# Values of two head pairs by seven products of blocks, and pairs that begin with the tokens the last one ended with

## The chip, the cores and the metric

The kernel runs on one core of one Trainium2 chip. The metric is the device time of one execution in microseconds, of which the median over several executions is taken; smaller is better. Everything is in 32-bit floats. In what follows PE is TensorE (the matmuls), PEld its loads of weights, DVE VectorE, ACT ScalarE, POOL GpSimd, and SP SyncE, whose queue issues most of the DMAs.

## What is computed

Two layers over x of shape (2, 512, 64, 32), that is two batches of 2048 tokens with 512 channels. Layer 0 is full softmax attention over eight heads of 64, whose queries and keys see an embedding of position beside the channels and whose values see the channels alone. Layer 1 is a Nystrom attention with a pseudo-inverse, followed by a linear map whose weights are looked up in a table of 16 levels. Only layer 0 is touched by the change:

```python
def _L0_conv_ref(hidden_states, Wq, Wk, Wv, Wout, bout):
    qk_hs = jnp.concatenate([hidden_states, emb], axis=1)
    qk_hs = qk_hs.reshape(B, -1, S).transpose(0, 2, 1)
    v_hs = hidden_states.reshape(B, C, S).transpose(0, 2, 1)
    q, k, v = qk_hs @ Wq, qk_hs @ Wk, v_hs @ Wv      # to 8 heads of 64
    scores = jnp.einsum('bhqd,bhkd->bhqk', q, k) * scale
    attn = jax.nn.softmax(scores, axis=-1)
    o = jnp.einsum('bhqk,bhkd->bhqd', attn, v)
    o = o.transpose(0, 2, 1, 3).reshape(B, S, HEADS * hd_v)
    o = o @ Wout + bout
    return o.transpose(0, 2, 1).reshape(B, C, H, W) + hidden_states
```

## The kernel before

**Tiling.** The unit of layer 0 is a pair of heads: 128 columns of each weight matrix. There are eight pairs, four for each batch, numbered 0 to 7 here and named (b, hp) in the code. The 2048 tokens of a batch stand in four blocks of 512 (`xbs`), channels in the partitions as four chunks of 128. A matmul of 32-bit floats shows as two instructions in the profile.

**Stages.** Stage n is `attention0` of pair n. It runs over 32 groups of two steps; a step is one block of 512 queries against 128 keys. For each step PE makes the scores (L1289), ACT the exponentials (L1297), DVE adds them up for the softmax's sums (L1307), and PE makes the product with the values (L1319) one group later. A block of queries ends every eight groups: ACT and DVE then read the two banks of the result out into the query tile (L1325, L1326), the next block's first product with the values needs the same two banks, PE sums the exponentials over the partitions (L805), DVE inverts (L1336), and SP spreads the inverse by eight DMAs (L816). The exponentials have six buffers, two for a group.

**What runs beside it.** The projections of pair n+1 are a generator, `Heads0.units`, that `attention0` advances in bursts: at the groups listed in `BURSTS[n]` it runs until the generator yields REST. Between bursts each group runs one thing: if the list `soon` holds a call, the first of it; otherwise, if the group stands in `TABLE[n]`, one step of `feed_forward_map`. That generator prepares layer 1's linear map in 84 steps: for each of four blocks the 16 levels, of which 14 cost two DVE instructions (L1397, L1398), and at the end four products on PE (L1411) and the load of the output weights `wo_f` into the buffer that these products read. Whatever is left of it after stage 3 is drained there, ahead of stage 4, whose burst at group 2 needs `wo_f`. `NVS` says how many steps run beside each block of values.

**Queries and keys by seven products.** For six of the eight pairs (all but (0,0) and (1,1), which are `plain`) `products` makes the queries and keys of two blocks of tokens by seven products of blocks where eight would be needed: the tokens' two halves of channels and two blocks of tokens are one 2x2 matrix of blocks, the key and query weights the other. It needs four sums of weights (`combine_w`, L1007 to L1010) and four sums of tokens (`Tokens.sum`, L917) for each half `tp` of the batch's tokens. The sums of tokens stand in four tiles (tags t5, t6, t7, t4) with one buffer each, so a half's sums replace the other's. `Tokens.begin` puts them on `soon`, or `need0` runs them when a product asks for one. Every pair goes through half 0, then half 1. The two banks of the tag "pp" hold a product that is read out by adds (`pc`) and a sum that stays in its bank over three products (`pu`).

**Values.** `values_of_tokens` (L1153) makes the values of one pair: for each block of 512 tokens four tiles of 128 tokens times four chunks of channels, with the tokens as PE's weights and 128 columns of the value weights moving; ACT copies the bank out (L1160). Per pair these are 64 matmuls, 128 instructions.

**Order.** PE, DVE, ACT and POOL run in the order in which the program is written; the order of SP's queue is made by the framework. A tag's buffers are given out as they come free. The tag "qo" has five, for the query tiles, which turn into the attention's output and stay until a batch's output projection; "k" and "v" have two each.

Of the kernel before, what the change touches and what calls it, by code (L numbers as in the profile page):

```python
# [37 lines left out]
def general_path(  # L38
# [636 lines left out]

PREFETCH = 26

TABLE = *[(1, 2, 3, 4, 5, 6, 7, 22, 23, 28)] * 3, (13, 14, 18, 19, 20, 21, 22, 23, 24, 26, 27, 28), (), (), (), ()
WAIT = 4
NVS = 3, 3, 3, 1  # L680
FEW = (2, 1), (1, 2), (1, 1), (2, 2)
BURSTS = (
    *[(9, 17, 25)] * 4, (2, 4, 7, 10, 12, 15, 18, 20, 23, 26, 28, 31),
    (9, 17, 25), (9, 17, 25), (9, 17),
)


# [1 line left out]
def fast_path(  # L689
# [63 lines left out]
    def chunked(ap):  # L753
        return ap.rearrange("(k p) n -> p k n", p=P)
# [64 lines left out]
    def advance(gens, n=1, whole=False):  # L819


        made, i = 0, 0
        while made < n and i < len(gens):
            got = next(gens[i], gens)
            if got is gens:
                gens.pop(i)
            elif got is GAP:
                i += 1
            elif got is REST:
                if whole:  # L830
                    break
            else:
                made += 1
        return made
# [53 lines left out]
    def blocks_of(w1, w2):  # L888

        lo, hi = slice(0, 2), slice(2, 4)  # L890
        return {1: w1[:, lo, :], 2: w1[:, hi, :], 4: w2[:, hi, :]}

    class Tokens:


# [6 lines left out]
        def begin(self):  # L902
            soon.extend(lambda m=m: self.sum(m) for m in (5, 6, 7, 4))
# [25 lines left out]
    def tokens_of(b, n, xbs, tp):  # L929
        return Tokens(f"{b}_{n}_{tp}", *xbs[2 * tp : 2 * tp + 2])  # L930

    class Heads0:


        def __init__(self, b, hp):
            self.b, self.hp = b, hp
            self.name = f"f0_{b}_{hp}"
            self.plain = (b, hp) in ((0, 0), (1, 1))
            self.n_units = 13 if b else 15 if self.plain else 14
            if self.plain:  # L940
                kinds = "qk" if b == 0 else "kq"
                self.uses = [(kind, t) for kind in kinds for t in range(NTB)]
            else:
                self.uses = [(kind, 2 * tp + t) for tp in range(2) for kind, t in (("k", 0), ("k", 1), ("q", 1), ("q", 0))]
            self.w, self.ws, self.e, self.ft = {}, {}, {}, {}

        def load(self, kinds="qk"):
            for kind in kinds:
                self.w[kind] = load_w0(kind, self.b, self.hp)

        def begin(self):
            self.k = kvpool.tile([P, S], F32, tag="k", name=f"k_{self.name}")
            self.v = kvpool.tile([P, NST, P], F32, tag="v", name=f"v_{self.name}")

        def queries(self):
# [43 lines left out]
        def combine_w(self):  # L999

            wk, wq = self.w["k"][0], self.w["q"][0]
            lo, hi = slice(0, 2), slice(2, 4)
            few = wpool0.tile([P, KC, P], F32, tag="s", name=f"s_{self.name}")
            s4 = wpool0.tile([P, 2, P], F32, tag="s4", name=f"s4_{self.name}")
            s1, s2, s3 = few[:, lo, :], few[:, hi, :], wq[:, lo, :]
            self.ws = {**blocks_of(wk, wq), 5: s1, 6: s2, 7: s3, 3: s4}
            nc.vector.tensor_tensor(s1, wq[:, lo, :], wq[:, hi, :], ALU.add)  # L1007
            nc.vector.tensor_tensor(s2, s1, wk[:, lo, :], ALU.subtract)
            nc.vector.tensor_tensor(s3, wk[:, lo, :], wq[:, lo, :], ALU.subtract)
            nc.vector.tensor_tensor(s4, wk[:, hi, :], s2, ALU.subtract)  # L1010

        def products(self, tp, part, after):

# [51 lines left out]
            yield  # L1065
            yield REST

        def values(self):
            for t in range(NTB):
                values_of_tokens(self.v, t, self.xbs[t], lambda k: self.w["v"][0][:, k, :], self.name)  # L1070
                yield

        def units(self, xbs, parts, after=None, ready=None):

            self.xbs = xbs
            self.begin()
            values = self.values()
            if self.b == 0 and self.plain:
                self.few("q")
                self.embed(4)  # L1080
                yield
            if self.plain:
                for i, (kind, t) in enumerate(self.uses):
                    if i == 2 and self.b == 0:
                        self.few("k")
                        self.embed(2)
                    if kind == "q" and self.b:
                        if t == 0:
                            yield from values
                            while not ready():  # L1090
                                yield GAP
                    if kind == "q" and t == 0:
                        self.queries()
                    self.project(kind, t)
                    yield
                if after:
                    after.begin()
            else:
                self.queries()
                if self.b and self.hp == 0:  # L1100
                    for m in range(2):
                        next(values)
                        advance(ffn_map, 3)
                        yield
                if not self.ws:
                    self.combine_w()
                    for _ in range(2):
                        next(values)
                        yield
                while ready and not ready():  # L1110
                    yield GAP
                for tp in range(2):
                    yield from self.products(tp, parts[tp], parts[1] if tp == 0 else after)
            if self.next:
                self.next.load()
                if self.next.b:
                    self.next.embed(4)
            for i, _ in enumerate(values):
                advance(ffn_map, NVS[i])
                yield  # L1120
                if self.next and not self.next.plain and not self.next.ws:
                    self.next.combine_w()
                if self.next and self.next.b == 0 and i == 2:
                    self.next.few("qk", nc.scalar.copy)
            if self.next:
                self.next.load("v")

            big = small.tile([P, 2], F32, tag="big0", name=f"big_{self.name}")
# [923 lines left out]
    made, plain = {}, lambda n: heads[n].plain  # L2052

    def parts_for(n):
        if n not in made:
            made[n] = [tokens_of(todo[n][0], n, xbs, tp) for tp in range(2)]
        return made[n]

    def units_of(n, ready=None):

        others = [m for m in range(n + 1, len(todo)) if todo[m][0] == todo[n][0] and not plain(m)]
        after = parts_for(others[0])[0] if others and not (n and plain(n)) else None
        return heads[n].units(xbs, None if plain(n) else parts_for(n), after, ready)

    loaded, ffn_map = [], [feed_forward_map()]
# [48 lines left out]
    def first_products():  # L2114
# [695 lines left out]
```

## Time and profile before

| what | value |
|---|---|
| median of 4 runs | 2650.52 us (2650.29 to 2650.92) |
| the profiled execution's own time | 2651.93 us |
| its span, first to last instruction | 2650.0 us |
| mean granted TensorE clock | 0.999 |
| scores L1289, 4096 instructions | 489.8 us busy |
| product with the values L1319, 4096 instructions | 494.1 us busy |
| values of layer 0, L1153 (vp_f), 1024 instructions | 117.9 us busy |
| sums of tokens L917, 48 instructions | 1218 ns each |
| adds of exponentials L1307 (two tiles), 448 instructions | 574.6 us busy |

The stages of layer 0 begin at 53.9, 207.3, 363.0, 515.8, 683.7, 904.0, 1056.6 and 1208.3 us, read from the first scores of each pair. Busy time of PE counts matmuls whose ends are modelled and overlap; durations of a group of matmuls are better read from the starts of the pieces in the chain of waits.

### The profile page before, as it was taken

The page shows a single profiled execution, that of the slowest core. Times are in us where ns is not written, and L with a number is a line of the kernel's source. Part 1 is how long each engine was busy: PE and PEld are TensorE (multiplying, and loading weights), DVE is VectorE, ACT ScalarE, POOL GpSimd, SP SyncE. Part 2 cuts the span into 40 slices and gives each one's busy share as a digit, 9 for nine tenths or more (in the row PEclk, how much of TensorE's full clock was granted, in tenths as well). Part 3 has the DMA queues.
Part 4 walks back from the last instruction along what each step waited for, and adds up shares of the span by engine and source line. Part 5 has one row for each costly group of instructions (what it writes and reads, how often), then busy time and mean ns, then how long its engine had stood idle before and what let it go on. Part 6 is the DMA issues. An engine that isn't in the chain of part 4 may idle for free.

```text
span 2650.0 us, 41440 instructions
## 1 busy us (share of the span) xinstructions
PE 2624.2 (99%) x16882; PEld 1353.5 (51%) x16882; DVE 1780.3 (67%) x2259; ACT 921.5 (35%) x1398; POOL 170.8 (6%) x127
## 2 busy tenths in 40 slices
PE   9999999999999999999999999999999999999998
PEld 5343443444344344353344555777677666665444
DVE  5788897886667777767868866544644645465665
ACT  1434453543344434435522323223333233231310
POOL 0011011000001100000002000000000000000000
PEclk9999999999999999999999999999999999999999
DMA  4001001201221201011115633213111113021211
GB/s 147 21 30 36 14 33 49 77 21 52 88 80 57 92 25 33 25 57 60 39 45 183 223 125 123 93 33 132 45 37 61 61 45 106 29 80 39 93 36 49
DMA packets 123609, 177.16 MB, mean 67 GB/s; under 512 B 16785, under 2 KB 77969, under 8 KB 120849
## 3 DMA queue, kind: packets, MB, share of 16 engines
q1 hardware_dynamic: 117264, 153.15, 17.6%
q0 software_dynamic: 5440, 20.97, 2.0%
q8 instruction: 134, 2.20, 0.3%
q14 instruction: 67, 0.54, 0.1%
q10 hardware_dynamic: 704, 0.31, 0.0%
HBM read 94.02 MB, written 63.57 MB: 59 GB/s over the span
## 4 chain that ended last, share of the span: by engine, by line
PE 92%; DVE 5%; issue 1%; ACT 1%; DMA 1%; SPq 0%; DVEq 0%; ACTq 0%
PE av_f L1319 15%; PE sc_f L1289 15%; PE pb L1866 5%; PE pa L1866 5%; PE vp_f L1153 4%; PE fp_g L2022 4%; PE yp_g L1168 4%; PE yp_f L1168 4%; PE vp L1153 4%; PE pc_f L1021 3%; PE pu L2207 3%; DVE acc_f L1307 2%; PE pu_f L1021 2%; PE sc L1695 2%; PE sc L1923 2%; PE av L1716 2%
## 5 line engine op out<-in xcount | busy, mean ns | idle before, releaser
L1297 ACT ACTIVATE p_f<-sc_f 128x1024 f32<-128x1024 f32 x512 | 496.7, 1022 | 539.9 <-PE sc_f L1289 539.8
L1307 DVE TENSOR_TENSOR acc_f<-acc_f,p_f 128x1024 f32<-128x1024 f32 x448 | 574.6, 1283 | 110.2 <-ACT p_f L1297 83.1
L1319 PE MATMUL av_f<-p_f,v_f 64*64 64x512 f32 x4096 | 494.1, 589 | 2.8 <-DVE q_f L1326 2.8
L1289 PE MATMUL sc_f<-q_f,k_f 64*64 64x512 f32 x4096 | 489.8, 591 | 0.3 <-ACT p_f L1297 0.3
L1319 PEld LDWEIGHTS av_f<-p_f,v_f 64*64 64x64 f32 x4096 | 162.4, 133 | 286.6 <-issue 274.1
L1289 PEld LDWEIGHTS sc_f<-q_f,k_f 64*64 64x64 f32 x4096 | 154.2, 133 | 282.2 <-issue 276.8
L1866 PE MATMUL pa<-M 128*128 128x192 f32 (+1 forms) x640 | 150.3, 380 | 0.0
L1866 PE MATMUL pb<-R 128*128 128x192 f32 (+1 forms) x640 | 149.3, 380 | 0.6 <-DVE M L1879 0.6
L1153 PEld LDWEIGHTS vp_f<-wv_f,x 128*128 128x128 f32 x1024 | 115.8, 192 | 5.5 <-issue 5.2
L1866 PEld LDWEIGHTS pb<-R 128*128 128x128 f32 x640 | 106.5, 190 | 23.6 <-DVE M L1879 0.8
L1866 PEld LDWEIGHTS pa<-M 128*128 128x128 f32 x640 | 108.2, 193 | 19.8 <-ACT M L1857 2.0
L1153 PE MATMUL vp_f<-wv_f,x 128*128 128x128 f32 x1024 | 117.9, 276 | 0.0
L1339 POOL TENSOR_TENSOR q_f<-q_f,rinv_f 128x512 f32<-128x512 f32 x32 | 51.9, 1621 | 968.1 <-DMA rinv_f<-acc_f 700.9
L1168 PE MATMUL yp_g<-o,wo_f 128*128 128x512 f32 x256 | 113.8, 595 | 0.0
L1168 PE MATMUL yp_f<-q_f,wo_f 128*128 128x512 f32 x256 | 112.4, 594 | 0.1
L1153 PE MATMUL vp<-w,xh 128*128 128x128 f32 x896 | 105.8, 276 | 0.0
L1153 PEld LDWEIGHTS vp<-w,xh 128*128 128x128 f32 x896 | 102.2, 192 | 5.4 <-issue 3.5
L1879 DVE SCALAR_TENSOR_TENSOR M<-M,pb 128x320 f32<-128x320 f32 (+1 forms) x160 | 60.1, 417 | 60.8 <-PE pb L1866 60.8
L2022 PE MATMUL fp_g<-xn_g,mT 128*128 128x512 f32 (+1 forms) x232 | 100.8, 586 | 0.0
L1928 ACT ACTIVATE p<-sc 128x512 f32<-128x512 f32 x128 | 66.7, 601 | 91.8 <-PE sc L1923 91.3
L1960 POOL TENSOR_TENSOR o<-o,rinv 128x512 f32<-128x512 f32 x32 | 44.5, 1389 | 774.8 <-DVE rinv L1959 573.9
L1879 DVE SCALAR_TENSOR_TENSOR R<-M,pa 128x320 f32<-128x320 f32 (+1 forms) x160 | 58.4, 406 | 42.0 <-PE pa L1866 42.0
(293 smaller groups left out, 3215.0 us busy)
## 6 DMA issues: line engine op xcount, KB each, us to landing
xh<-xh_fd SPq DMA_DIRECT2D x12, 1024.0 KB, 8.2
rinv_f<-acc_f SPq DMA_DIRECT2D x256, 32.0 KB, 1.9
xr_f<-in_x_dram SPq DMA_DIRECT2D x8, 1024.0 KB, 5.3
x_fd<-xr_f POOLq DMA_DIRECT2D x8, 1024.0 KB, 4.7
xh_fd<-xn_f POOLq DMA_DIRECT2D x8, 1024.0 KB, 4.4
k_fd<-kq SPq DMA_DIRECT2D x16, 512.0 KB, 2.6
q_fd<-kq SPq DMA_DIRECT2D x16, 512.0 KB, 3.1
k<-k_fd SPq DMA_DIRECT2D x8, 1024.0 KB, 6.0
```

The lines of the kernel that those rows point to most:

```text
L1021: nc.tensor.matmul(to, lhsT=w[:, k, :], rhs=x[:, k, :], start=start and k == 0, stop=k == 1, skip_group_check=True,)
L1153: nc.tensor.matmul(vp[:, j * P : (j + 1) * P], lhsT=xb[:, k, j * P : (j + 1) * P], rhs=w_of(k), start=k == 0, stop=k == KC - 1,)
L1168: nc.tensor.matmul(yp, lhsT=wo_sb[:, k, m * P : (m + 1) * P], rhs=oTs[k][:, toks], start=k == 0, stop=k == NPAIR - 1,)
L1289: nc.tensor.matmul(sc[r * D : (r + 1) * D, h, :], lhsT=hd.k[rows, lo : lo + D], rhs=hd.q[rows, t * TB : (t + 1) * TB], start=True, stop=True,)
L1297: nc.scalar.activation(p, sc, AF.Exp, scale=D**-0.5)
L1307: nc.vector.tensor_tensor(acc, first if c == 1 else acc, p, ALU.add)
L1319: nc.tensor.matmul(av[r][half, :], lhsT=hd.v[keys, c, half], rhs=pp[keys, h, :], start=c == 0, stop=c == NST - 1,)
L1866: nc.tensor.matmul(dst, lhsT=lhsT[:, k, t * P : (t + 1) * P], rhs=rhs[:, k, :], start=k == 0, stop=k == 1)
L1879: nc.vector.scalar_tensor_tensor(out, m, scale, pr, ALU.mult, ALU.subtract)
L1928: nc.scalar.activation(p[:, h, :], sc, AF.Exp, scale=D**-0.5)
L2022: nc.tensor.matmul(fp[:, cols], lhsT=mT[:, k, m * P : (m + 1) * P], rhs=self.xn[:, k, cols], start=k == 0, stop=k == KC - 1,)
L2207: nc.tensor.matmul(to, lhsT=w[:, k, :], rhs=x[:, k, :], start=start and k == 0, stop=k == 1, skip_group_check=True)
```

## The change

Four pairs of layer 0 are joined into two couples, (0,1) with (0,2) and (1,2) with (1,3). The first of a couple makes the values of both, again by seven products of blocks in place of eight: the tokens' blocks and their sums are those that its queries and keys use, and the value weights of the two pairs are the other matrix (`values_of_two`, `sums_of_blocks`, `combine_v`). The second has no values to make. The couple's two value weights, their sums, and the second pair's values stand in tiles of the tag "qo"; a tile of layer 1 that stood there moves to the tag "v". Each couple's products and values alternate by half, so that a half's sums serve both.

A pair now begins with the half of the tokens whose sums are still there: (0,2) and (1,2) go through half 1 first, and `parts_for` hands on the half that the pair before ended with. The last half of a pair therefore no longer starts the next pair's sums.

`TABLE` and `BURSTS` get other entries, and map steps run beside the couple's values, one for each of their units. The sums of weights of some pairs are put on `soon` in place of being made in a burst.

```diff
-TABLE = *[(1, 2, 3, 4, 5, 6, 7, 22, 23, 28)] * 3, (13, 14, 18, 19, 20, 21, 22, 23, 24, 26, 27, 28), (), (), (), ()
+TABLE = (1, 2, 3, 4, 6, 7), (1, 2, 3, 4, 5, 6, 7, 8, 10, 11, 12, 18, 19, 20, 21, 22, 23, 26, 27, 28), (1, 2, 3, 4, 5, 6, 7, 10, 11, 12, 20, 21, 22, 23, 24, 27, 28), (13, 14, 18, 19, 20, 21, 22, 23, 24, 26, 27, 28), (), (), (), ()
 BURSTS = (
-    *[(9, 17, 25)] * 4, (2, 4, 7, 10, 12, 15, 18, 20, 23, 26, 28, 31),
-    (9, 17, 25), (9, 17, 25), (9, 17),
+    (5, 9, 17, 25), (9, 17, 25), (9, 17, 25), (9, 17, 25), (2, 4, 7, 10, 12, 15, 18, 20, 23, 26, 28, 31),
+    (9, 14, 20, 25), (9, 17), (9, 17),
 )
+    def sums_of_blocks(w1, w2, few, s4):
+        lo, hi = slice(0, 2), slice(2, 4)
+        s1, s2, s3 = few[:, lo, :], few[:, hi, :], w2[:, lo, :]
+        nc.vector.tensor_tensor(s1, w2[:, lo, :], w2[:, hi, :], ALU.add)
+        nc.vector.tensor_tensor(s2, s1, w1[:, lo, :], ALU.subtract)
+        nc.vector.tensor_tensor(s3, w1[:, lo, :], w2[:, lo, :], ALU.subtract)
+        nc.vector.tensor_tensor(s4, w1[:, hi, :], s2, ALU.subtract)
+        return {**blocks_of(w1, w2), 5: s1, 6: s2, 7: s3, 3: s4}
...
+            self.couple = (b, hp) in ((0, 1), (1, 2))
+            self.coupled = (b, hp) in ((0, 2), (1, 3))
+            self.order = (1, 0) if (b, hp) in ((0, 2), (1, 2)) else (0, 1)
...
+        def load_v(self):
+            if self.couple:
+                w = qopool.tile([P, S], F32, tag="qo", name=f"wv_{self.name}")
+                w = w.rearrange("p (j k n) -> p j k n", j=4, k=KC)
+                for j in range(2):
+                    cols = slice((self.hp + j) * P, (self.hp + j + 1) * P)
+                    nc.sync.dma_start(w[:, j], chunked(wv0[:, cols]))
+                w1, w2, few, s4 = (w[:, j] for j in range(4))
+                self.vs = (w1, w2, few, s4[:, :2, :])
+                self.wvs = {}
+            elif not self.coupled:
+                self.load("v")
...
         def begin(self):
             self.k = kvpool.tile([P, S], F32, tag="k", name=f"k_{self.name}")
+            if self.coupled:
+                return
+            if self.couple:
+                v = qopool.tile([P, S], F32, tag="qo", name=f"v_{self.next.name}")
+                self.next.v = v.rearrange("p (c d) -> p c d", d=P)
...
+        def values_of_two(self, tp, part, after):
...
+            def product(to, m, start=True):
+                while m not in part.of or m not in self.wvs:
+                    soon.pop(0)()
+                w, x = self.wvs[m], part.of[m]
+                for j in range(TB // P):
+                    cols = slice(j * P, (j + 1) * P)
+                    for k in range(2):
+                        nc.tensor.matmul(
+                            to[:, cols], lhsT=x[:, k, cols], rhs=w[:, k, :],
+                            start=start and j + k == 0, stop=k == 1, skip_group_check=True,
+                        )
...
+            def begin(i, t, bank):
+                nc.scalar.copy(piece(i, t), blocks(bank))
+            def add(i, t, bank):
+                d = piece(i, t)
+                nc.vector.tensor_tensor(d, blocks(bank), d, ALU.add)
+            pc = other(2)
+            begin(0, 0, pc)
+            pu = bank(f"pu_{name}")
+            product(pu, 1)
+            add(0, 0, pu)
+            yield
+            pc = other(5)
+            begin(0, 1, pc)
+            begin(1, 1, pc)
+            product(pu, 6, False)
+            add(0, 1, pu)
+            yield
+            pc = other(3)
+            add(0, 1, pc)
+            product(pu, 7, False)
+            add(1, 1, pu)
+            yield
+            pc = other(4)
+            begin(1, 0, pc)
+            add(1, 0, pu)
+            if after:
+                after.begin()
+            yield
+            yield REST
...
-                for tp in range(2):
-                    yield from self.products(tp, parts[tp], parts[1] if tp == 0 else after)
+                if self.couple:
+                    soon.append(self.combine_v)
+                for tp in self.order:
+                    then = parts[1 - tp] if tp == self.order[0] else after
+                    steps = self.products(tp, parts[tp], None if self.couple else then)
+                    if self.coupled and tp != self.order[0]:
+                        steps = (step for step in steps if step is not REST)
+                    yield from steps
+                    if self.couple:
+                        values = self.values_of_two(tp, parts[tp], then)
+                        if tp == self.order[0]:
+                            for step in values:
+                                if step is not REST:
+                                    advance(ffn_map, 1)
+                                yield step
             if self.next:
                 self.next.load()
                 if self.next.b:
                     self.next.embed(4)
-            for i, _ in enumerate(values):
-                advance(ffn_map, NVS[i])
+                if not self.next.ws and not self.next.plain and (self.coupled or self.b and self.plain):
+                    soon.append(self.next.combine_w)
+            if self.coupled:
+                values = ()
+            if self.coupled and self.next:
+                yield REST
+                self.next.few("qk", nc.scalar.copy)
+                yield
+            for i, step in enumerate(values):
+                if step is REST:
+                    continue
+                advance(ffn_map, 1 if self.couple else NVS[i])
                 yield
...
             if self.next:
-                self.next.load("v")
+                self.next.load_v()
...
     def parts_for(n):
         if n not in made:
             made[n] = [tokens_of(todo[n][0], n, xbs, tp) for tp in range(2)]
+            before = [m for m in made if m < n and todo[m][0] == todo[n][0]]
+            if before:
+                tp = heads[n].order[0]
+                made[n][tp] = made[before[-1]][tp]
         return made[n]
...
-        others = [m for m in range(n + 1, len(todo)) if todo[m][0] == todo[n][0] and not plain(m)]
-        after = parts_for(others[0])[0] if others and not (n and plain(n)) else None
+        after = parts_for(1)[0] if n == 0 else None
...
             else:
-                d = qopool.tile([P, S], F32, tag="qo", name=f"kq_{pair.name}_{tp}")
+                d = kvpool.tile([P, S], F32, tag="v", name=f"kq_{pair.name}_{tp}")
```

More of the change, by code (lines that the diff above doesn't have):

```diff
@@ L943, in __init__ @@
             else:
-                self.uses = [(kind, 2 * tp + t) for tp in range(2) for kind, t in (("k", 0), ("k", 1), ("q", 1), ("q", 0))]
+                self.uses = [(kind, 2 * tp + t) for tp in self.order for kind, t in (("k", 0), ("k", 1), ("q", 1), ("q", 0))]
             self.w, self.ws, self.e, self.ft = {}, {}, {}, {}
@@ L1004, in combine_w, with combine_v @@
             s4 = wpool0.tile([P, 2, P], F32, tag="s4", name=f"s4_{self.name}")
[L1005 to L1010, printed above, removed]
+            self.ws = sums_of_blocks(wk, wq, few, s4)
+        def combine_v(self):
+            self.wvs = sums_of_blocks(*self.vs)
         def products(self, tp, part, after):
@@ L1066, in products, with other, piece, blocks @@
             yield REST
+        def values_of_two(self, tp, part, after):
+            name = f"v_{self.name}_{tp}"
+            def product(to, m, start=True):
[9 more added lines that the diff above has]
+                        )
+            def other(m):
+                to = bank(f"pc{m}_{name}")
+                product(to, m)
+                return to
+            def piece(i, t):
+                v, t = (self.next.v if i else self.v), t + 2 * tp
+                return v[:, 4 * t : 4 * t + 4, :]
+            def blocks(bank):
+                return bank.rearrange("p (j d) -> p j d", d=P)
+            def begin(i, t, bank):
[27 more added lines that the diff above has]
+            yield REST
         def values(self):
```

## The prediction

> **What bounds the kernel now.** I read the page first: the busy shares, the slices, the shares of the chain that ended last.
>
> ```profile
> PE 2624.2 (99%) x16882; PEld 1353.5 (51%) x16882; DVE 1780.3 (67%) x2259; ACT 921.5 (35%) x1398; POOL 170.8 (6%) x127
> ...
> DVE  5788897886667777767868866544644645465665
> ...
> PE 92%; DVE 5%; issue 1%; ACT 1%; DMA 1%; SPq 0%; DVEq 0%; ACTq 0%
> ```
>
> TensorE (PE) is busy all the time and makes up 92% of the chain; VectorE (DVE) is the second load, nowhere denser than in layer 0 (the first 18 slices). Since ends of matmuls are modelled, I take rates from the chain in order of time, where each piece starts where the last one let it:
>
> ```profile
> 247.53 1.72 PE pc_f L1021 x4
> 249.25 1.72 PE pu_f L1021 x4
> ...
> 326.48 10.93 PE vp_f L1153 x96
> 338.67 3.77 PE vp_f L1153 x32
> 342.44 1.88 PE sc_f L1289 x16
> 344.31 1.72 PE av_f L1319 x16
> ...
> 480.69 14.49 PE vp_f L1153 x128
> ```
>
> A pair's values (vp_f, 128 instructions) cost 14.49 us, 113.2 ns each, and nothing stands between them. One of the seven products (four instructions over 512 columns) takes 1.72 us, 429 ns for four times the columns; so 128 columns cost about a quarter of 512, and TensorE goes by columns. Removing a column removes time, as long as VectorE doesn't take over. Whether it can, the windows by stage say. Stage n is the attention of pair n with the projections of pair n+1 beside it; columns: stretch, length, then busy us of PE, PEld, DVE, ACT, POOL.
>
> ```profile
> 53.90:207.30 153.40, 151.65 (x1221) 64.31 (x1224) 127.89 (x136) 68.26 (x77) 17.18 (x12) 1.00 0.11 34
> 207.30:363.00 155.70, 154.10 (x1248) 65.49 (x1244) 133.41 (x145) 68.64 (x78) 18.40 (x12) 1.00 0.09 28
> 363.00:515.80 152.80, 152.04 (x1248) 64.83 (x1244) 129.34 (x143) 68.26 (x76) 10.80 (x8) 1.00 0.17 54
> 515.80:683.70 167.90, 167.29 (x1280) 70.37 (x1276) 124.56 (x128) 70.71 (x80) 6.59 (x4) 1.00 0.16 50
> ...
> 904.00:1056.60 152.60, 152.60 (x1241) 64.68 (x1244) 121.16 (x110) 68.26 (x76) 11.06 (x6) 1.00 0.13 37
> 1056.60:1208.30 151.70, 151.70 (x1244) 64.61 (x1240) 106.02 (x93) 68.26 (x76) 6.04 (x6) 1.00 0.15 49
> ```
>
> VectorE fills 83 to 86% of stages 0 to 2 (127.89/153.40, 133.41/155.70). It is no bound on the average, but it runs in order, and where it is late at the wrong moment TensorE stops. The timeline of stage 0 shows the one kind of place:
>
> ```profile
> 165.34 0.42 DVE L1397 TENSOR_SCALAR hits_f<-tmp_f 128x512 f32<-128x512 f32 x1
> ...
> 165.79 0.69 DVE L1398 TENSOR_TENSOR wl_f<-wl_f,hits_f 128x512 f32<-128x512 f32 x1
> 166.21 1.03 PE L1319 MATMUL av_f<-p_f,v_f 64*64 64x512 f32 x4
> 166.40 1.22 DVE L1307 TENSOR_TENSOR acc_f<-p_f,p_f 128x1024 f32<-128x1024 f32 x1
> 167.54 0.68 DVE L1326 TENSOR_TENSOR q_f<-av_f,q_f 128x512 f32<-128x512 f32 x1
> 168.28 1.93 PE L1319 MATMUL av_f<-p_f,v_f 64*64 64x512 f32 x12 [1.04 <-DVE q_f L1326]
> ```
>
> At the switch from one 512-token block to the next, the attention's values need the bank that q_f (L1326) reads out. A map step (L1397, L1398) stood ahead of it on VectorE, and TensorE waited: 16 instructions and their switch take 1.90 us in undisturbed rows, here 166.21 to 170.14 (where the sums L805 start), so 2.0 us were lost. The same happens at 323.98 and 639.14.
>
> **The change, part by part.**
>
> (1) Values of two pairs. Removed for each couple: 2 pairs x 128 = 256 instructions. Added: 2 halves of the tokens x 7 products x 4 token tiles x 2 chunks x 2 passes = 224, of the same form. For two couples that is 64 fewer x 113.2 ns = **-7.25 us**. By stage: stages 0 and 5 gain 96 x 113.2 ns = 10.9 us, stages 1 and 6 lose 14.5 us. A product now ends every 16 instructions, a block before every 32. What such a hand-over costs the trace doesn't show for 128 columns. Below: nothing, since L1021's products follow each other at 4 x 429 ns, with the same two banks. Above: what the entry into a burst costs, 1.91 - 1.72 = 0.19 us (pc_f at 284.31 against its neighbours), for 28 products, 5.3 us. I take +0.3, near the L1021 rows.
>
> (2) Its VectorE and ScalarE work. Per couple 10 adds from a bank at 692 ns (L1041, the same shapes) = 6.9 us, and 4 sums of weights at 417 to 426 ns = 1.7 us; ScalarE keeps 8 copies of 586 ns. All of it lies beside products of 1.8 us each: between two uses of a bank there is always one whole product, and the longest read-out of a bank is two copies, 1.2 us. Nothing on the path; without that cover 0.6 us per hand-over.
>
> (3) Tokens kept. Pairs 2, 3, 6, 7 start with the half that the last ended with, so 4 x 4 token sums (L917, 1218 ns) go: 19.5 us of VectorE, against (2) 17.2 us. These sums fill stages 0, 1, 3 and 5 in the groups after a burst, so what they free is slack, not path, except at the switch above.
>
> (4) Map steps moved. A step is about 0.45 + 0.71 = 1.15 us (L1397, L1398). Counting the groups in which something in `soon` comes first: before, stages 0 to 3 take 16, 20, 20, 18 of the 84 steps after 10 ahead of stage 0; after, 9, 14, 24, 22. VectorE by stage, from the windows: stage 0: 127.9 - 4.9 (sums) + 8.6 (2) - 7 x 1.15 = 124 of 163; stage 1: 133.4 - 4.9 - 6 x 1.15 = 122 of 141; stage 2: 129.3 + 4 x 1.15 = 134 of 153; stages 5 and 6 under 125 of 163 and 101 of 137. The fullest is 88%. In stage 0 nothing is left in groups 18 to 24 ahead of the last switch, so the 2.0 us at 168.28 goes: **-2.0**, and with no step at group 28 most of the 0.48 us that the sums waited for VectorE at 211.41: **-0.4**. Late next there is only the exp's own add. In stage 1 the sums of weights and five steps stand where four sums and two steps stood: the stall of 323.98 stays, between -0.5 and +0.5, take 0. Stage 2 now has four steps ahead of its last switch: 0 to +1.0, take +0.2. In stage 0 the sums of the values' weights and a step follow a burst just before the first switch: 0 to +1.0, take +0.3.
>
> (5) Bursts. Stages 0 and 5 have four instead of three, stage 6 two: one more in all. Stage 1's third holds only two small embedding products, which before sat among the values. Entry 0.19 + exit (1.88 - 1.72) 0.16 = **+0.35**.
>
> (6) The map's own products. My count leaves five steps, four products and the last, for the drain at the end of stage 3 (before: 648.83 and 666.25). TensorE does them either way. But they now stand right ahead of stage 4, and the load of wo_f, which writes where they read, is issued after them, behind or beside the 1 MB store of the product (landing 6.7 and 8.5 us). The first yp_f comes 11.1 us after the stage's first scores (683.66 to 694.80), so 6.7 + 0.4 is hidden; xr_f, queued on SP behind the store, lands at 0.6 + 8.5 + 4.9 = 14 us and is needed at 11.1 + 3.7. Margins of 4 and 1 us: 0 to +3 if SP's queue puts the eight rinv_f pieces (4.9 us) ahead; take +0.3.
>
> (7) Buffers. The couple's weights and the second pair's values stand among the q tiles, layer 1's first kq in a v tile: slots that nobody waits for in the trace. 0.
>
> **Sum.** -7.25 + 0.3 - 2.0 - 0.4 + 0.2 + 0.3 + 0.35 + 0.3 = **-8.2 us**. The profiled execution took 2651.93 us (span 2650.0 and 1.9 around it), so 2643.7; it lies 1.4 above the median of the runs, so **2642.3** for the median.
>
> [...]
>
> **Rivals.**
>
> *A, it is given back (nothing to measure).* Stage 1 loses its whole burst of values, the stretch in which ten map steps ran beside 14.5 us of TensorE; now all its steps share groups with the adds. A group gives VectorE 3.43 us and asks 2 x 1.28 + 1.15 = 3.7, so each step adds 0.27 us of lag; eight in a row give 2. If the first switches of stages 1 and 2 and the last of stage 2 stall for 1 us each, and wo_f or xr_f costs 3 at stage 4: -8.2 + 6 = -2.2, **2648.3**. Against it: stages 1 and 2 have seven such steps in a row already, and their first switch shows 0.2 us (16 av_f instructions in 1.93 instead of 1.72 us at 241.40).
>
> *B, VectorE becomes the bound of layer 0 (slower).* The place is the switch again: four in each of stages 0 to 3, three of the 16 stall now. If lag is never worked off, all stall at 2.0 us each: 13 x 2.0 = 26, with (1) alone kept, 2650.5 - 7.25 + 26 = **2669**. It decides from (5.3 + 7.25) / 2.0, some six new stalls. For it: the fuller map steps and the lost burst. Against it: 122 to 134 us of work in 141 to 163.
>
> *C, banks (slower).* If every new product waits for the copy before it, 28 x 0.59 = 16.5: 2658.8. L1021's products, with longer read-outs (2 x 0.69 us), show no gap.
>
> **How the numbers follow.** The forecast (faster by over 0.2%, that is under 2645.2; 0.2% is about what runs of this kernel can tell from no change) gets 0.80, A 0.13, B 0.05, C 0.02. The forecast's own range: the low ends (no hand-over cost, -0.5 in stage 1, no other stall) give 2640.5, and another stall may go with the sums, so 2639.5; the high ends of (4) and (6) together 2647. The whole range is 2639.5 to 2647: it holds the forecast and the nearer part of A. Faster 0.80, same 0.13, slower 0.07.
>
> **What would show it.** Values instructions down from 1024 to 960, 448 of them in the new products, and L917 from 48 to 32. Stage 0 near 162 us, stage 1 near 141, 5 near 163, 6 near 137. No wait of av_f on q_f at stage 0's last switch. Wrong would be: pieces of the new products above 1.85 us (step 1), waits of av_f on VectorE in stages 1 and 2 above 1 us (step 4), yp_f or the first residual waiting for a DMA at stage 4 (step 6).

## The result, and the profile after

The changed kernel takes 2652.9 us (median of 40 runs, 2650.62 to 2656.29) against 2650.28 for the kernel before (60 runs beside them, 2648.4 to 2652.5): ratio 1.0011, 95% interval 1.0007 to 1.0016. It is slower by 2.6 us, where 8.2 us less were forecast. Its profiled span is 2653.0 us, at a mean granted clock of 0.997 (before 0.999); that execution took 2654.88 us, 2.0 above the median, and what follows on stages and waits is read from it.

The page of the changed kernel: busy shares, the slices of VectorE, the shares of the chain that ended last.

```profile
PE 2622.1 (99%) x16818; PEld 1351.4 (51%) x16818; DVE 1783.5 (67%) x2271; ACT 921.1 (35%) x1398; POOL 172.3 (6%) x127
...
DVE  5769897988467766787867866644644645465665
...
PE 93%; DVE 5%; ACT 1%; DMA 1%; issue 1%; SPq 0%; DVEq 0%; ACTq 0%
```

The 64 instructions are gone (16818 for 16882) and little else on this page moves: the page can't show where the time went. The windows by stage can (stretch, length, busy us of PE, PEld, DVE, ACT, POOL, granted clock, DMA share, GB/s).

```profile
54.00:217.00 163.00, 162.33 (x1317) 75.21 (x1320) 122.11 (x126) 70.58 (x81) 14.41 (x11) 1.00 0.07 23
217.00:360.80 143.80, 139.88 (x1124) 51.01 (x1120) 125.25 (x130) 66.37 (x74) 19.73 (x14) 1.00 0.10 34
360.80:515.30 154.50, 152.85 (x1248) 64.59 (x1244) 132.41 (x151) 68.24 (x76) 11.35 (x8) 1.00 0.18 56
515.30:682.10 166.80, 166.80 (x1276) 70.71 (x1268) 131.72 (x148) 69.99 (x79) 7.14 (x4) 1.00 0.11 31
902.50:1074.00 171.50, 168.44 (x1337) 76.69 (x1340) 125.21 (x119) 70.59 (x80) 11.03 (x6) 0.97 0.11 32
1074.00:1211.50 137.50, 137.50 (x1116) 52.99 (x1112) 107.80 (x95) 65.89 (x72) 6.77 (x5) 1.00 0.18 54
```

Taken from the first scores of each pair, the lengths of stages 0 to 6 and of the rest are:

| kernel | 0 | 1 | 2 | 3 | 4 | 5 | 6 | rest |
|---|---|---|---|---|---|---|---|---|
| before | 153.5 | 155.7 | 152.7 | 167.9 | 220.3 | 152.7 | 151.7 | 1441.7 |
| after | 163.1 | 143.7 | 154.5 | 166.9 | 220.4 | 171.5 | 137.5 | 1441.5 |

Stages 0, 3, 4 and 6 are near what was forecast (162, no change, no change, 137), stages 1 and 2 are 2.5 and 1.5 us longer than forecast, and stage 5 is 8 us longer (171.5 for 163). It is also the one whose clock is not 1.00. The signs of being wrong that the prediction named did not show: behind the first product of each block the new products take 1.79 us, av_f waits in stages 1 and 2 for 0.52 us at most, and TensorE shows no wait in stage 4. The time went where no sign had been set.

**The new products are as cheap as forecast.** Pieces of the chain of waits in order of time (start, us):

```profile
184.32 1.79 PE pu_v_f L1109 x16
186.11 1.79 PE pc_v_f L1109 x16
187.89 1.79 PE pu_v_f L1109 x16
```

Each starts where the one before let it: 1.79 us for 16 instructions, 111.9 ns each, no hand-over. (The first of each of the four blocks takes 1.98, the entry that step (5) priced at 0.19; the one behind the embedding products takes 2.00.)

**Stage 5.** The timeline of the changed kernel at its first block of queries (start, us, engine, line, operation, in brackets the idle time before and its releaser):

```profile
914.72 1.22 DVE L1344 TENSOR_TENSOR xn_f<-xn_f,rstd_n 128x1024 f32<-128x1024 f32 x1
...
915.69 1.38 POOL L1452 TENSOR_TENSOR q_f<-q_f,rinv_f 128x512 f32<-128x512 f32 x1 [35.72 <-DMA rinv_f<-acc_f]
915.85 5.60 DVE L1420 TENSOR_TENSOR acc_f<-acc_f,p_f 128x1024 f32<-128x1024 f32 x2
...
917.03 3.34 POOL L1343 TENSOR_TENSOR xn_f<-xn_f,rstd_n 128x1024 f32<-128x1024 f32 x1
...
921.38 0.41 DVE L897 TENSOR_TENSOR s_f<-wq_f 128x256 f32<-128x256 f32 x1
...
922.50 0.42 DVE L900 TENSOR_TENSOR s_f<-wk_f,s_f 128x256 f32<-128x256 f32 x1
...
925.30 2.28 DVE L1244 TENSOR_REDUCE big_f<-k_f 128x1 f32<-128x2048 f32 x1
...
939.27 0.68 DVE L1439 TENSOR_TENSOR q_f<-av_f,q_f 128x512 f32<-128x512 f32 x1
...
940.01 3.68 PE L1432 MATMUL av_f<-p_f,v_f 64*64 64x512 f32 x12 [3.06 <-DVE q_f L1439]
```

And the kernel before at the same place:

```profile
918.82 2.20 POOL L1339 TENSOR_TENSOR q_f<-q_f,rinv_f 128x512 f32<-128x512 f32 x1 [36.28 <-DVE acc_f L1307]
...
917.32 2.55 DVE L1307 TENSOR_TENSOR acc_f<-acc_f,p_f 128x1024 f32<-128x1024 f32 x2
...
919.79 2.28 DVE L1131 TENSOR_REDUCE big_f<-k_f 128x1 f32<-128x2048 f32 x1
...
922.10 1.25 DVE L1136 SCALAR_TENSOR_TENSOR bound<-big_f 128x1 f32<-128x1 f32 x1
...
937.38 2.79 PE L1319 MATMUL av_f<-p_f,v_f 64*64 64x512 f32 x16
...
937.50 0.69 DVE L1326 TENSOR_TENSOR q_f<-av_f,q_f 128x512 f32<-128x512 f32 x1
```

Two things load VectorE more ahead of the first switch. The four sums of the query and key weights (L897 to L900, 921.38 to 922.92) now stand on `soon` here. And the two multiplications of GpSimd (L1452, L1343) now run beside two adds of exponentials, which take 5.60 us in place of 2.55; before, they began at 918.82 and met the reduction, which kept its 2.28 us, and the small bound operation (1.25 us for 0.16). In this stage a group asks VectorE for two adds, 2.66 us, and gives it 3.43, so that only 0.77 us of lag is worked off in each. Counted from the stage's first scores, VectorE reads the bank out at 36.76 us, before at 33.52. At the switch, TensorE (PE) is idle for 3.06 us; the kernel before shows no idle row there, though its 16 instructions take 2.79 us for the 1.90 of undisturbed rows. Then something is late that no count of instructions shows; granted clock in the column before the last two:

```profile
936.00:938.00 2.00, 0.94 (x8) 0.06 (x2) 1.90 (x2) 1.24 (x2) 0.00 (x0) 1.00 0.00 0
938.00:940.00 2.00, 0.00 (x0) 0.00 (x0) 2.00 (x4) 0.00 (x0) 0.00 (x0) 0.78 0.00 0
940.00:942.00 2.00, 1.99 (x10) 0.77 (x12) 1.90 (x2) 0.00 (x0) 0.00 (x0) 0.50 0.00 0
...
946.00:948.00 2.00, 2.00 (x3) 0.67 (x2) 0.00 (x0) 0.00 (x0) 0.00 (x0) 0.50 0.00 0
...
950.00:952.00 2.00, 2.00 (x6) 0.95 (x5) 0.69 (x1) 0.00 (x0) 0.00 (x0) 1.00 0.48 131
```

The clock falls to half at about 939.1 and comes back at about 949.3: 10.2 us, in which the 12 instructions take 3.68 us (1.93 at the full clock).

**Stage 0's end**, the second place. The timeline of the changed kernel around the last burst of stage 0:

```profile
197.12 0.69 DVE L1131 TENSOR_TENSOR v_f<-pu_v_f,v_f 128x512 f32<-128x512 f32 x1 [2.01 <-ACT v_f L1127]
...
198.79 2.28 DVE L1244 TENSOR_REDUCE big_f<-q_f 128x1 f32<-128x2048 f32 x1
...
200.99 1.74 DVE L1449 RECIPROCAL acc_f<-acc_f 128x256 f32<-128x256 f32 x1
...
207.44 16.70 DVE L1420 TENSOR_TENSOR acc_f<-acc_f,p_f 128x1024 f32<-128x1024 f32 x10
...
212.41 4.01 POOL L1013 TENSOR_TENSOR e_k_f<-ft_k_f 128x512 f32<-128x512 f32 x2
...
224.19 0.64 PE L805 MATMUL rs_f<-acc_f,ones 128*32 128x256 f32 x8 [3.53 <-DVE acc_f L1420]
```

The last add of the values ends at 197.8, after the burst's last product (from 196.40 PE is at scores again), and a map step, the queries' reduction and the reciprocal, which the program puts behind it, are done at 202.7, with the exponentials' adds waiting. GpSimd's multiplication at 210.36 and its embedding adds (L1013, 2.0 us each) then slow the adds: ten take 16.70 us where 13.2 would do (1.33 us from one to the next). The embedding adds end at 220.4, just ahead of the sums; in the kernel before the same four end at 202.6, 8.8 us ahead of them. The sums wait 3.53 us; before 0.48:

```profile
211.41 0.64 PE L805 MATMUL rs_f<-acc_f,ones 128*32 128x256 f32 x8 [0.48 <-DVE acc_f L1307]
```

The wait forecast to go, av_f on q_f at stage 0's last switch, is gone.

### The profile page after: what moved, and what is told of

Read it like the earlier page. It is cut to its first block, busy times and chain, and to the rows that moved or that the text cites. A ratio compares the mean times of both kernels' runs of the same rounds, so it can differ in the third digit from the quotient of the medians.

```text
span 2653.0 us, 41334 instructions
## 1 busy us (share of the span) xinstructions
PE 2622.1 (99%) x16818; PEld 1351.4 (51%) x16818; DVE 1783.5 (67%) x2271; ACT 921.1 (35%) x1398; POOL 172.3 (6%) x127
## 4 chain that ended last, share of the span: by engine, by line
PE 93%; DVE 5%; ACT 1%; DMA 1%; issue 1%; SPq 0%; DVEq 0%; ACTq 0%
PE av_f L1432 16%; PE sc_f L1402 16%; PE pa L1979 5%; PE pb L1979 5%; PE fp_g L2135 4%; PE yp_g L1281 4%; PE yp_f L1281 4%; PE vp L1266 4%; PE pc_f L1051 3%; PE pu L2324 3%; PE pu_f L1051 2%; PE sc L1808 2%; PE vp_f L1266 2%; PE av L1829 2%; PE sc L2036 2%; PE av L2052 2%
## 5 line engine op out<-in xcount | busy, mean ns | idle before, releaser
L1452 POOL TENSOR_TENSOR q_f<-q_f,rinv_f 128x512 f32<-128x512 f32 x32 | 51.2, 1599 | 990.2 <-DMA rinv_f<-acc_f 759.2
L2041 ACT ACTIVATE p<-sc 128x512 f32<-128x512 f32 x128 | 66.7, 602 | 91.6 <-PE sc L2036 91.2
L2330 ACT COPY kq<-pu 128x512 f32<-128x512 f32 x56 | 32.2, 586 | 154.7 <-PE pu L2324 124.4
L1817 ACT ACTIVATE p<-sc 128x512 f32<-128x512 f32 x128 | 67.2, 625 | 42.7 <-PE sc L1808 42.7
```

The costliest lines, as they stand in the source:

```text
L1817: nc.scalar.activation(p[:, h, :], scs[h], AF.Exp)
```

## The experiments

Diffs are against the changed kernel but where another is named. Ratios are to the kernel before, run on the same chip, with the 95% interval.

**e1: the sums of pair (1,2)'s weights back in the burst.**

```diff
-if not self.next.ws and not self.next.plain and (self.coupled or self.b and self.plain):
+if not self.next.ws and not self.next.plain and self.coupled:
     soon.append(self.next.combine_w)
...
-for _ in range(2):
+for _ in range(0 if self.couple else 2):
     next(values)
```

> The changed kernel, with the four sums of pair (1,2)'s query and key weights made at the start of its first burst instead of ahead of stage 5's first groups. Theory (VectorE is late at stage 5's first switch, because 1.7 us of sums now stand ahead of it): the wait of 3.1 us and the stretch at half clock behind it (939 to 949 us, some 4.5 us) go, stage 5 falls from 171.5 to about 164, the time by 7 to 8 us to 2645. Rival (the products of the values are slower than worked out, or the lost burst of stage 1 costs it): nothing changes at stage 5, 2653.

2649.65 us, 1.0001 (0.9992 to 1.001); stage 5 takes 169.0. The direction is right and the size is not: the two adds beside GpSimd still take 5.61 us, TensorE is still idle for 1.80 us, and the half clock lasts 6.8 us.

```profile
917.17 5.61 DVE L1420 TENSOR_TENSOR acc_f<-acc_f,p_f 128x1024 f32<-128x1024 f32 x2
...
939.32 0.69 DVE L1439 TENSOR_TENSOR q_f<-av_f,q_f 128x512 f32<-128x512 f32 x1
...
940.06 3.19 PE L1432 MATMUL av_f<-p_f,v_f 64*64 64x512 f32 x12 [1.80 <-DVE q_f L1439]
```

At this switch e1 has the same work on VectorE as the kernel before, and differs by what GpSimd overlaps: the two adds (5.61 us for 2.55) in place of the bound (0.16 for 1.25). The read-out comes at 35.49 us of the stage for 33.52: 1.97 us later by the overlap alone. The sums of weights add the other 1.27 of the changed kernel's 3.24.

**e2: the queries' reduction ahead of the values.**

```diff
+if self.couple:
+    most(0, self.q)
 for i, step in enumerate(values):
...
-most(0, self.q)
+if not self.couple:
+    most(0, self.q)
```

> The changed kernel, with the first pair of each couple reducing its queries (2.28 us of VectorE) before its last values instead of behind them. Theory (the values' last adds hold the reduction and the reciprocal back behind the end of the burst, so that stage 1 begins late): the 3.7 us that the sums of pair 0's last block lose at 224 us fall to about 1.3, stage 0 and 1 together lose 2 to 2.5 us, time about 2650.5. Rival (the lag comes from GpSimd's four embedding adds, beside which the adds of exponentials take 1.88 instead of 1.23 us): no more than 0.5 us gained.

2649.4 us, 0.9996 (0.9987 to 1.0005). The idle time ahead of the sums falls from 3.53 to 1.34 us and stage 1 from 143.7 to 141.4, as expected; stage 5 stays at 171.5, with the same half clock of 10.2 us.

```profile
221.04 0.64 PE L805 MATMUL rs_f<-acc_f,ones 128*32 128x256 f32 x8 [1.34 <-DVE acc_f L1423]
```

**e4: the sums of pair (1,2)'s weights on `soon`, in the kernel before.** The first hunk keeps that pair's two blocks of values at the start of its burst.

```diff
+if self.b and self.hp == 2:
     for _ in range(2):
         next(values)
...
 self.next.embed(4)
+if self.b and self.plain:
+    soon.append(self.next.combine_w)
```

> The kernel before, with this one edit: the four sums of pair (1,2)'s query and key weights are put among the calls of stage 5's first groups, as the change does; its first two blocks of values stay at the start of the first burst. [...]

2655.79 us, 1.0023 (1.0014 to 1.0032): 5.7 us slower with nothing else changed, and of the stages it is stage 5 that grows (159.1 for 152.7, with a half clock of 6.8 us). The timeline at its switch:

```profile
919.46 1.50 DVE L1007 TENSOR_TENSOR s_f<-wq_f 128x256 f32<-128x256 f32 x1
920.99 2.47 DVE L1008 TENSOR_TENSOR s_f<-s_f,wk_f 128x256 f32<-128x256 f32 x1
923.38 0.41 DVE L1009 TENSOR_TENSOR wq_f<-wk_f,wq_f 128x256 f32<-128x256 f32 x1
...
941.21 3.68 PE L1322 MATMUL av_f<-p_f,v_f 64*64 64x512 f32 x12 [3.13 <-DVE q_f L1329]
```

Here the sums themselves meet GpSimd's multiplications (918.51 to 923.2): the first two take 1.50 and 2.47 us, the third, beside nothing, 0.41.

**e5: the keys' reduction and the bound behind the first switch**, the sums left where the change put them.

```diff
+if self.b and self.plain:
+    soon.extend([lambda: None] * 8)
 soon.append(both_of_them)
```

> The changed kernel, with the sums of weights left where they are and the reduction of pair (1,1)'s keys with its bound (2.28 + 0.16 us of VectorE) put off to behind stage 5's first burst. Theory (what counts is the sum of VectorE's work ahead of the switch, not which): the wait at 940 us goes as in the run with the sums in the burst, 2645. Rival (the sums of weights wait for their weights' DMA, or their place itself matters): the wait stays, 2653 less 0.5 at most.

2647.7 us, 0.9991 (0.9982 to 1.0001); stage 5 takes 164.8, idle 0.86 us, with no half clock there.

```profile
938.32 1.93 PE L1434 MATMUL av_f<-p_f,v_f 64*64 64x512 f32 x12 [0.86 <-DVE q_f L1441]
```

Taking 2.44 us of other work off VectorE ahead of the switch does more than taking the 1.7 us of sums off (e1): it is the load there, not the sums as such. The time expected, 2645, was not reached: 0.86 us of the wait is left, and this execution has 3.4 us of half clock in stage 1.

**e6: e1, e2 and e5 together.**

> The changed kernel with the three edits of the first runs together: sums of pair (1,2)'s weights in its first burst, queries of a couple's first pair reduced before its last values, reduction of pair (1,1)'s keys behind stage 5's first burst. Theory (the change's gain was right, and two pile-ups of VectorE gave it back): stage 5 at 163.5 to 164, stages 0 and 1 together 2.3 shorter, no half clock in layer 0, 2642 to 2643. Rival (something else holds stage 5 or the couple's stages back): 2646 or more, as the better of the single edits.

2642.84 us, 0.997 (0.9959 to 0.9982). Stages 1 and 5 take 141.3 and 163.5, as forecast for the change itself. One execution of each kernel at stage 5's first switch:

| kernel | TensorE idle | half clock | stage 5 | over e6 |
|---|---|---|---|---|
| after | 3.06 | 10.2 | 171.5 | 8.0 |
| e1 | 1.80 | 6.8 | 169.0 | 5.5 |
| e5 | 0.86 | none | 164.8 | 1.3 |
| e6 | none | none | 163.5 | 0 |

The idle rows understate a wait, as the ends of matmuls are modelled. In e6 the 16 instructions at the switch still take more than the undisturbed 1.90 us:

```profile
932.79 2.57 PE L1437 MATMUL av_f<-p_f,v_f 64*64 64x512 f32 x16
```

**e11: the clock kept, the wait kept.** The changed kernel with matmuls in the idle time whose result nobody reads.

```diff
+if n == 5 and i // GROUP == 9:
+    busy = bank("busy")
+    for _ in range(12):
+        nc.tensor.matmul(busy[:, :P], lhsT=mean_w, rhs=mean_w, start=True, stop=True)
```

> The changed kernel, with 12 small matmuls (24 instructions, about 2.7 us) into a bank of their own put ahead of the product with the values that waits at stage 5's first switch. They add TensorE work and compute nothing that is used. Theory (TensorE's idle wait of 3.1 us halves its clock for 10 us, which costs 5 us of the 8 that stage 5 lost): the wait is filled, the clock stays, stage 5 falls from 171.5 to 166 to 167, time 2647 to 2648. Rival (the half clock costs nothing, since VectorE is the one that is late there): 2653, or later by the added work.

2649.98 us, 0.9998 (0.9989 to 1.0007); stage 5 takes 167.0. Its timeline:

```profile
935.13 2.94 PE L1471 MATMUL busy<-mean_w 128*128 128x128 f32 x24
938.01 3.04 PE L1432 MATMUL av_f<-p_f,v_f 64*64 64x512 f32 x16
...
941.54 1.98 PE L1051 MATMUL pc_f<-x,wk_f 128*128 128x512 f32 x4
```

The read-out still comes as late (36.74 us into the stage for 36.76), but four instructions of the projections take 1.98 us (3.78 in the changed kernel). Of stage 5's 8.0 us over e6 the half clock is 171.5 - 167.0 = 4.5, the wait itself 3.5. The stage is as expected; the time is not, 2649.98 for 2647 to 2648. The execution shown took 2647.49. The runs at a mean clock of 0.999 took 2647.49 to 2649.39, those at 0.997 and 0.998 took 2649.77 to 2651.25; which wait brought their half clock no trace shows.

**e7: e6, and the embedding adds of GpSimd inside the burst.**

```diff
 self.next.few("qk", nc.scalar.copy)
+self.next.embed(4)
...
-if self.next and self.next.b == 0:
+if self.next and self.next.b == 0 and self.plain:
     soon.append(lambda: self.next.embed(4))
```

> The run with all three edits, and GpSimd's four embedding adds issued inside the burst that makes their inputs, in place of two groups after it. Theory (GpSimd slows VectorE's adds of exponentials from 1.23 to 1.88 us while it runs, five of them, 3.3 us a stage, and this is what is left of the waits at the ends of stages 0 and 1, 1.5 and 1.3 us): these waits fall to 0.3 to 0.5, 2640 to 2641. Rival (the adds only meet GpSimd somewhere else): the same time as with the three edits, within 1 us.

2639.32 us, 0.9956 (0.9943 to 0.997): 11.8 us under the kernel before on that chip, the largest gain of all runs (e10 and e12 lie within its interval). Its timeline at the end of stage 0:

```profile
194.44 2.19 POOL L1013 TENSOR_TENSOR e_k_f<-ft_k_f 128x512 f32<-128x512 f32 x2 [29.33 <-ACT ft_k_f L996]
...
196.58 2.23 POOL L1013 TENSOR_TENSOR e_q_f<-ft_q_f 128x512 f32<-128x512 f32 x2
...
205.74 14.07 DVE L1428 TENSOR_TENSOR acc_f<-acc_f,p_f 128x1024 f32<-128x1024 f32 x10
```

Where VectorE waits for TensorE, GpSimd's adds take 1.1 us each in place of 2.0, and the ten adds of exponentials 14.07 in place of 16.70. In stages 0 to 6, TensorE shows no wait on VectorE any more (before: five, 3.5 us in all).

**e8: the order of the halves alone.** `couple` and `coupled` false, `TABLE`, `BURSTS` and the tag of the kernel before, with e1's edit: 16 sums of tokens fewer, TensorE's work as before.

> The tokens' order alone: every pair makes its own values by the old blocks, with the tables, the bursts and the place of the sums of weights of the kernel before, but the pairs begin with the half whose sums are there. VectorE has 16 sums of tokens less (19.5 us), TensorE the same work as before. Theory (sums after the second burst are what made av_f wait at the last switches of stages 0, 1 and 3, 2.0, 1.5 and 1.4 us before): these go, 2645 to 2647. Rival (VectorE's work in the groups off the path is worth nothing): 2650.

2644.41 us, 0.9977 (0.9968 to 0.9986). Stages 0, 1 and 3 lose 2.1, 1.5 and 1.7 us: the waits at their last switches are gone. This was priced as part of step (4), at -2.4; alone it is worth 6.7 (3.7 to 8.5 by the interval, 5.3 by the stages of the profiled executions), for 19.5 us of VectorE's work that counted as slack.

**e9: e6 with the tokens not kept** (`if before:` made `if False:`, and the next pair's first half begun early as in the kernel before).

> The run with all three edits, but every pair makes the sums of tokens anew for each half, and the last half of a pair puts the next pair's first four sums among the calls again: 19.5 us more of VectorE, TensorE unchanged. Theory (the couples' gain needs the room that the kept sums make): the sums fall into the last groups of stage 0 and the groups after the second burst of the others, the waits at the ends of stages 0, 1 and 5 grow, slower by 4 to 9 us than the three edits, 2647 to 2651. Rival (the couples stand alone): within 1.5 us of it.

2667.14 us, 1.0064 (1.005 to 1.0077): 24.3 us over e6, several times what was expected. The sums at the end of stage 0 wait 5.68 us; and the token sums on `soon` took the groups of map steps, which were left over at the end of stage 3:

```profile
685.42 15.01 PE L1529 MATMUL mp<-wff_f,wl_f 128*128 128x512 f32 x28 [13.21 <-DMA wff_f<-in_wffT_dram]
```

Stage 3 takes 183.1 for 166.9. The load of wff_f is issued at 680.3 us, behind the drained steps (in e6 at 643.4), and TensorE waits 13.2 us; the clock is at half from 677.3 to 690.9, 5.5 us of it after the wait. Stages 1 and 6 take 7.1 and 1.7 us more than in e6: these 8.8 are the waits that were expected (4 to 9), and stage 3's 16.2 come from the map steps left over, as the tables were not filled anew. So with these tables the couples need the kept tokens; how much of it other tables would save, no run shows.

**e10: one couple only**, (1,2) with (1,3); stages 0 to 3 as in e8, with e1's and e5's edits.

> The tokens' order of the run with the order alone, and only the second batch's couple, pairs (1,2) and (1,3), where VectorE has no map steps; its sums of weights in the first burst and pair (1,1)'s keys reduced behind it. Theory (the couple's saving of 3.6 us arrives in full where VectorE has room, and it is stages 0 to 3 that give theirs back to map steps, late reductions and GpSimd): stages 5 and 6 at 163.5 and 137.5, 3.3 to 3.6 us faster than the order alone, about 2641. Rival (the couple costs in itself, by its banks, adds or bursts): 2643 to 2645.

2640.61 us, 0.9968 (0.9955 to 0.9981), with 163.5 and 137.5 in stages 5 and 6 (152.6 and 151.7 in e8): -3.3 us of the 3.6 counted, where VectorE has room. The other couple, e6 against e8, makes stage 0 longer by 11.7 and stage 1 shorter by 12.9 (by count 10.9 and 14.5), and stages 2 and 3 longer by 1.7 and 0.7: in e6 nothing is left of it. In e7 stages 0 to 3 are 1.8 us shorter together than in e8.

**e12: e7 with map steps moved** from stage 2's first groups to stage 0's (19, 20, 21).

> The run with the embedding adds in the burst, with three map steps moved from groups 5 to 7 of stage 2 to groups 19 to 21 of stage 0, where nothing stands ahead of the last switch. Theory (stage 2's first switch waits, 0.5 and 0.4 us, for the lag of seven steps in a row): 0.5 to 1 us faster than that run, about 2638.5. Rival (the steps cost in stage 0 what they free in stage 2): the same time.

2640.48 us, 0.9962 (0.9949 to 0.9975), no gain on e7 (on another chip): stage 2 gains 1.4 us, stage 1 loses 1.1 at its last switch.

## Why the prediction was wrong

**Step (1)** was right: 64 instructions fewer, 111.9 ns each, no hand-over (0.3 was taken). With the waits away, stages 5 and 6 of e10 show -3.3 of the 3.6 us counted for a couple.

**Step (2), "Nothing on the path", failed.** The argument was that between two uses of a bank there is always one whole product. That holds within a burst (no product waits), and not at its end: the last add on VectorE ends behind the last product, and what the program puts behind that add starts late by as much. Forecast 0; e2 measured 2.3 us for the order alone. Taking GpSimd's adds away gave e7 a further 3.5 (against e6), at the ends of stages 0 and 1 together; not all of that is the change's doing, as the sums waited there in the kernel before too (0.48 and 0.76 us; in e6 1.34 and 1.12).

**Step (4) failed at stage 5**, where it mattered most: "stages 5 and 6 under 125 of 163 and 101 of 137". Stage 5's busy time came out near the forecast (125.21 us; stage 6's 107.80 is 7 above) and decided nothing. That the sums of weights move to `soon` was known, and step (4) followed the switches of stages 0 to 2 one by one, where map steps stand; stage 5 got the average alone, though the wait is one of a place. At its first switch the kernel before had no room left (2.79 us for 1.90). There the read-out came 3.24 us later: 1.97 by GpSimd's multiplications falling on the adds, which no step had as a term, and 1.27 by the sums of weights. That became 3.06 us of idle TensorE and 8.0 us with the clock. e4 shows the sums alone, which there meet GpSimd themselves, to cost 5.7.

**The price of a wait** was taken as its length in every rival. In these runs it isn't: the half clock was 4.5 of stage 5's 8.0 us. Rival B had the mechanism and not the size: it asked for some six new stalls of 2 us each to reach no gain, and two long ones, with the clock, were enough to pass it.

**Step (3)** was sized too small: kept tokens were called slack "except at the switch above", which took -2.4 with step (4); e8 shows -6.7. The waits at the last switches of stages 1 and 3, which the prediction let stand, went as well. What e6 reaches, 2642.84, is near the 2642.3 forecast, but by other terms, so that is luck: -6.7 from the order and -1.6 from the couples with their work on VectorE put elsewhere (too little for the intervals to tell from nothing), where the sum had -7.25 for the couples' products.

**The rest.** Stage 4 takes 220.4 for 220.3, so the 0.3 of step (6) was not needed; nothing showed against (5) and (7), which no run tried alone; rival C's bank waits didn't come.

**What stays open.** Why the last piece of rinv_f lands earlier in stage 5, which brings GpSimd's multiplications onto the adds. It is issued 11.1 us into the stage in every run; it lands at 12.9 in the changed kernel and in every run that has the first couple, at 14.3 to 14.5 in the kernel before, e4, e8 and e10. So it comes with the first couple or its tables; by what way, no run shows.

## What to carry to other kernels

Work of an engine "off the path" is to be costed at each place where the bounding engine takes something from it, with everything that stands ahead in its queue, and not by its share of a stage. Don't price a wait of the bounding engine by its length alone: 1.80 us of idle time brought a half clock of 6.8 us in e1, and 3.53 us brought none in the changed kernel. Take load off the nearly full engine first (the order of the halves alone gave 6.7 us); work saved on the bounding engine is paid out where the other one has room, as one couple alone did.

## What the runs showed of the hardware

**The clock.** The granted clock fell to 0.50 for 10.2 us in the changed kernel (TensorE idle for 3.06 us), for 6.8 in e1 (1.80), 6.8 in e4 (3.13) and 13.6 in e9 (13.2); the stretch began 2.2, 2.3, 3.0 and 5.1 us after the wait did. After 0.86 (e5) and 1.34 us (e2) the clock stayed at 1.00. The same 3.53 us at the end of stage 0 brought no half clock in the changed kernel's profile, and 3.4 us of it in e1's and e5's, where that place is the same code. And in layer 1 of the kernel before the clock is 0.50 for 3.4 us from 2475.1 on, where no idle row of the 15 us ahead is longer than 0.79 us. So the length of one wait does not settle it.

**GpSimd beside VectorE.** At stage 5's start an add of 128x1024 takes 1.225 us alone and 2.3 to 3.2 us beside GpSimd's two multiplications (the changed kernel); a reduction of 128x2048 keeps its 2.28 us beside them (the kernel before), while the bound operation there takes 1.25 us in place of 0.16. GpSimd's add of 128x512 takes 2.0 us beside adds of VectorE (the changed kernel) and 1.1 without them (e7). Why the adds and the bound operation are slowed and the reduction is not, no run shows.
